# A transformer pair's head: keys and values ahead of a norm's products, a root that nobody reads, and VectorE work moved later

## The chip, the cores and the metric

The kernel runs on one core of a Trainium2 chip. The core has a matrix engine (TensorE, PE in the profile, with PEld for its weight loads), VectorE (DVE), ScalarE (ACT), GpSimd (POOL) and SyncE (SP), which issues the transfers. The metric is the device time of one execution in microseconds. All arithmetic is in 32-bit floats.

## The reference

Two blocks run one after the other on 32 sequences of 64 positions with 512 features. The first is an attention block with an MLP, both behind a root-mean-square norm whose scale depends on the sequence's condition vector; the second is a sparse attention block behind a conditioned layer norm. What this case touches is the start of the first block:

```python
n = x * rsqrt(mean(square(x), -1) + 1e-6)       # ada_rms, twice: before attention, before the MLP
h = n * (w * (1.0 + t @ tw.T))[:, None, :]
q, k, v = h @ Wq.T, h @ Wk.T, h @ Wv.T          # 8 query heads of 64, one key/value head
q, k = apply_rope(q, pos_ids), apply_rope(k, pos_ids)     # cos and sin of pos * inv_freq
x = x + (softmax(q @ k.T / 8) @ v) @ Wo.T
h = ada_rms(x, time_emb, ln2_w, ln2_tw)
x = x + (silu(h @ Wg.T) * (h @ Wu.T)) @ Wd.T
```

## The kernel before, in words

The 2048 rows are cut into eight units of 256 (four sequences each). A unit passes through `attention0`, `mlp` and `attention1`. The MLP's products use a seven-product scheme of half-sized blocks, so each weight set (gate, up or down of one of eight column groups q) needs, beside its three loaded blocks and a fourth loaded apart (`a_n`), four sums of them. These sums are formed once, while unit 0's MLP runs: `sums_of_set` (L283 to L290) does three on VectorE and the fourth on GpSimd (all four on GpSimd for sets 0 and 1). Then they are stored in DRAM for the later units (`done_with`, L292). There are five set buffers (tag `mw`) and two for `a_n` (tag `a21`), so a later load waits until an earlier set is used up.

**Order.** A scheduler places the instructions of each engine from their dependencies, and each engine runs its own list in order. In the head of the kernel TensorE's order is written by hand: the string `FIRST` (L49) is a list of turns. `a` is one step of unit 0's attention, `b` one of unit 1's, `m` one of the condition's modulation products, `i` a pair of filler products (`idle(2)`, products of a constant tile that nobody reads), `|` takes a mark. A mark is the VectorE instruction emitted last at that turn. `after(tc, engine, mark)` gives whatever is emitted inside it on that engine an order behind the mark. Sets 2 to 4 get their sums behind `marks[0]` (L280), and the rotation angles of units 2 and 3, `angles(2)`, a chain of 35 VectorE instructions and two sines, stand behind `marks[1]` (L1113). After the head the planner `Order` mixes the jobs.

**The norm in the lean form** (units 0 and 1): ScalarE squares x (`rms`, L536), VectorE and GpSimd scale x into h by the condition, TensorE sums the squares into a short tile with products against ones (`root_by_quarters`, L508), ScalarE takes the root (L505) and VectorE the reciprocal (L506); for the MLP's norm the result is spread over the partitions again by products (`row_b`, L773) and multiplied into h (L558). In unit 0 four filler products stand between the norm's products `ms_a` and the key and value products `kv` (L656 to L659). The third unit's attention (`a2`) begins with such squares too; the scheduler places them on ScalarE in the head.

ScalarE evaluates functions from tables: where the next function is in another set of tables, an ACT_TABLE_LOAD stands before it.

Of the kernel before, what the change touches and what calls it, by code (L numbers as in the profile page):

```python
# [12 lines left out]
AF = mybir.ActivationFunctionType  # L13
# [4 lines left out]
P = 128  # L18
# [26 lines left out]
TURN = (0.15911865234375, 3.628432750701904e-05, 6.4192136051133275e-09, 1.4247115856860781e-12)  # L45
ROUND = 12582912.0
WARM = 11
STAY = 14103
FIRST = "aaaaaaa bb a mm aa bb a bbb | aa b mm a bb aa a m b a bi m b ii a b |".replace(" ", "")  # L49
EARLY = 4  # L50

LAST = "aa b aa b iii b aa ii b bb bbb aaaa aa bb aaaa bbbb bb bbbb".replace(" ", "")
# [46 lines left out]
@contextmanager  # L99
def ordered(tc, engine):  # L100

    traced = tc.nc.cur_bb.bb.instructions
    start = len(traced)
    yield
    mine = [i for i in traced[start:] if i.engine == engine]
    info = mybir.DependencyInfo(mybir.DependencyClass.NoSync, mybir.DependencyReason.DATA)
    for one, other in zip(mine, mine[1:]):
        tc.add_manual_dep(other, one.name, info, reason="order")


def latest(tc, engine):
    return next(i for i in reversed(tc.nc.cur_bb.bb.instructions) if i.engine == engine)


@contextmanager
def after(tc, engine, mark):

    traced = tc.nc.cur_bb.bb.instructions
    start = len(traced)
    yield  # L120
    info = mybir.DependencyInfo(mybir.DependencyClass.NoSync, mybir.DependencyReason.DATA)
    for one in [i for i in traced[start:] if i.engine == engine]:
        tc.add_manual_dep(one, mark.name, info, reason="order")
# [3 lines left out]
def two_blocks(ctx: ExitStack, tc: tile.TileContext, a: dict, out: bass.AP):  # L127
    nc = tc.nc
# [14 lines left out]
    def abank(name):  # L143
        tags = homes["now"]
        homes["n"] += 1
        return bank(tags[homes["n"] % len(tags)], name)


    stays = {"all": const.tile([P, STAY], F32, tag="stays", name="stays"), "at": 0}

    def fixed(shape):
        n, i = int(np.prod(shape[1:])), stays["at"]
        stays["at"] += n
        assert stays["at"] <= STAY
# [16 lines left out]
    def idle(n):  # L171

        idles["n"] += 1
        ps = abank(f"idle_{idles['n']}")
        for _ in range(n):
            nc.tensor.matmul(ps[:, :P], ones, ones, start=True, stop=True)
# [12 lines left out]
    nc.gpsimd.memset(eps0, EPS0)  # L189
    eps1 = fixed([P, 1])  # L190
    nc.gpsimd.memset(eps1, EPS1)
    quarter = fixed([P, 1])
    nc.gpsimd.memset(quarter, float(np.float32(np.pi / 2)))

# [78 lines left out]
                nc.sync.dma_start(t[:, 0:4], kept[i])  # L273
            sets[n] = t

    marks = []

    def combine(n):

# [152 lines left out]
    def spread_out(ps, of):  # L432

        for b in range(US):
            nc.tensor.matmul(ps[..., b, :], spread[:, b], of, start=True, stop=True)  # L435
# [43 lines left out]
    def space(room, tag, columns, name):  # L479

        if tag in room:
            return room[tag].pop(0)[:, :columns]
        if tag == "few":
            return work({"0": "tot0", "1": "kr1"}[room["ring"]], [P, columns], name, 1)
        return work(tag + room["ring"], [P, columns], f"{name}", RING.get(tag, RING.get(tag + room["ring"], 1)))

    def tile4(room, tag, name):
        return space(room, tag, KC * UT, name).rearrange("p (c t) -> p c t", t=UT)

    def total_of(room, t, name):  # L490

        total = space(room, "tot", UT, f"tot_{name}")
        nc.gpsimd.tensor_tensor(t[:, 0:2], t[:, 0:2], t[:, 2:4], ALU.add)
        nc.gpsimd.tensor_tensor(total, t[:, 0], t[:, 1], ALU.add)
        return total

    def mean_of(parts, name):

        ps = abank(name)
        for k, part in enumerate(parts):  # L500
            nc.tensor.matmul(ps[:, :UT], ones, part, start=(k == 0), stop=(k == len(parts) - 1))
        return ps[:, :UT]

    def inverse_root(mean, eps, r):
        nc.scalar.activation(r, mean, AF.Sqrt, bias=eps)  # L505
        nc.vector.reciprocal(r, r)  # L506

    def root_by_quarters(parts, eps, r, name):  # L508

        ps = abank(name)  # L510
        for k, part in enumerate(parts):
            for b in range(US):
                nc.tensor.matmul(
                    ps[b * HALF0 : (b + 1) * HALF0, :S],
                    ones[:, :HALF0],
                    part[:, b * S : (b + 1) * S],
                    start=(k == 0),
                    stop=(k == len(parts) - 1),
                )
        inverse_root(ps[:, :S], eps, r)  # L520
# [10 lines left out]
    def rms(u, s, h, room, name):  # L531

        x = x_units[u]
        lean = "lean" in room
        sq = tile4(room, "h", f"sq_{name}") if lean else work("sq", [P, KC, UT], f"sq_{name}", 1)
        nc.scalar.activation(sq, x, AF.Square)  # L536
        if lean:
            parts = [sq[:, k] for k in range(KC)]
            c = KC // 2

            for e, part in ((nc.gpsimd if name == "a0" else nc.vector, slice(0, c)), (nc.gpsimd, slice(c, KC))):
                to = h[:, part].rearrange("p c (b s) -> p c b s", s=S)
                of = x[:, part].rearrange("p c (b s) -> p c b s", s=S)
                by = s[:, part, US * u : US * (u + 1)].unsqueeze(3).to_broadcast([P, c, US, S])
                e.tensor_tensor(to, of, by, ALU.mult)
            yield 0.0, 1.5
        else:
            parts = [total_of(room, sq, name)]
            nc.gpsimd.tensor_tensor(by_seq(h), by_seq(x), per_seq(s, u), ALU.mult)
            yield 0.0, 6.0  # L550
        if lean:
            return parts
        r = space(room, "r", UT, f"r_{name}")
        inverse_root(mean_of(parts, f"ms_{name}"), eps0, r)
        return r
# [4 lines left out]
    def project(ps, w, cols, h):  # L560
        for k in range(KC):
            nc.tensor.matmul(ps, w[:, k, cols], h[:, k, :], start=(k == 0), stop=(k == KC - 1))  # L562
# [62 lines left out]
    def attention0(u, room, early=None, late=None):  # L625
# [4 lines left out]
        def query(i):  # L630

            q = abank(f"q0_{u}_{i}").rearrange("p (c t) -> p c t", c=2)
            for c in range(2):
                project(q[:, c], wqkv[i], slice(c * P, (c + 1) * P), h)
            two = [P, 2, UT]

            def turn(cos, sin):
                cos, sin = (t.unsqueeze(1).to_broadcast(two) for t in (cos, sin))
                rotate(qT[:, 2 * i : 2 * i + 2], q, cos, sin, two, f"q0_{u}_{i}")

            return turn

        def keys_values():
            kv = abank(f"kv0_{u}")
            project(kv[:, :UT], wqkv[0], slice(2 * P, 3 * P), h)
            return kv
# [5 lines left out]
        r = yield from norm  # L652
        kv, turn = None, None
        if lean:
            few = space(room, "few", 3 * S, f"quarters_{u}").rearrange("p (k c) -> p k c", c=S)
            root_by_quarters(r, eps0, few[:, 0], f"ms_a{u}")  # L656
            if u == 0:
                idle(4)
            kv = keys_values()  # L659
            yield 1.7, 0.0  # L660
            turn = query(0)
            yield 3.4, 0.0

        if lean:
            cos, sin, r = tables_by_quarters(u, few, room)
# [9 lines left out]
        kv = kv or keys_values()  # L675
# [89 lines left out]

        h = work("h2", [P, KC, UT], f"h2_{u}", 2)
        r = yield from rms(u, s0b, h, room, f"b{u}")
        if lean:
            root = space(room, "r", UT, f"r_b{u}")[:, :S]
            root_by_quarters(r, eps0, root, f"qs_b{u}")  # L770
            yield 0.3, 2.0
            r = abank(f"row_b{u}")[:, :UT]
            spread_out(r.rearrange("p (b s) -> p b s", s=S), root)  # L773
# [336 lines left out]
    first = work("p0", [P, 1024], "p0_0", 1)  # L1110

    def later_angles():
        with after(tc, mybir.EngineType.DVE, marks[1]):  # L1113
            angles(2)

    ahead = Job(attention0(1, {"ring": "1", "lean": True}, late=later_angles), A0)
# [5 lines left out]
    with ordered(tc, mybir.EngineType.PE):  # L1122
        for name in FIRST:
            if name == "i":
                idle(2)
            elif name == "|":
                marks.append(latest(tc, mybir.EngineType.DVE))
            else:
                next(streams[name], None)
    rest = [ahead]  # L1130
# [167 lines left out]
```

## Time and profile before

| what | value |
|---|---|
| three runs | 1037.51, 1037.50 and 1035.31 us (median 1037.5) |
| profiled execution | 1038.5 us, its span 1036.7 us |
| mean granted clock of TensorE | 0.995 |
| busy: TensorE, its weight loads | 1007.9 us, 939.0 us |
| busy: VectorE, ScalarE, GpSimd | 547.7 us, 332.1 us, 437.3 us |
| moved by DMA | 198.55 MB, mean 192 GB/s |

A line of a group or a time list names the start, the duration, the engine, the line in the kernel, the operation, the tiles written and read, the shape, how many, and in brackets the idle time before it with what ended it. One fp32 product shows as two matrix records. A wait for several things is put down to the one that came last. The chain of waits is followed back from the last instruction of a stretch; its lines have a start, a duration and what ran. The lines of stretches give busy time and instruction count of PE, PEld, DVE, ACT and POOL, then the granted clock, the DMA share and GB/s.

### The profile page before, as it was taken

How to read it: one execution, taken by the hardware profiler on the slowest of the kernel's cores; microseconds unless marked ns; L12 is line 12 of the kernel's file. 1: busy time of each engine (PE TensorE's matmuls, PEld its weight loads, DVE VectorE, ACT ScalarE, POOL GpSimd, SP SyncE). 2: the span in 40 equal slices, each digit the busy share in tenths (PEclk: the TensorE clock that was granted, in tenths of full speed). 3: DMA queues.
4: the chain of work that ended last, by engine and by line, in shares of the span. 5: the costliest groups of instructions: out<-in, count | busy, mean ns of one | idle time of the engine just before them, and what ended most of it. 6: DMA issues, size and time to landing. Idle time of an engine off the chain costs nothing.

```text
span 1036.7 us, 21605 instructions
## 1 busy us (share of the span) xinstructions
PE 1007.9 (97%) x8602; PEld 939.0 (91%) x8602; DVE 547.7 (53%) x1376; ACT 332.1 (32%) x683; POOL 437.3 (42%) x522
## 2 busy tenths in 40 slices
PE   8999999999999999999999999999999999999997
PEld 7788999998999988999999989899999899999986
DVE  5876646545355376444563366552565425553274
ACT  4442112254213342143340342342333522334042
POOL 5334445444245532345342354333563343644351
PEclk9999999999999999999999999999999999999999
DMA  9736896462765463672646645446754547666201
GB/s 329 257 104 219 289 305 238 143 214 108 235 209 195 152 214 132 230 250 102 228 168 224 244 143 192 165 147 234 245 198 150 181 167 263 221 214 214 93 1 42
DMA packets 68851, 198.55 MB, mean 192 GB/s; under 512 B 7312, under 2 KB 16272, under 8 KB 68368
## 3 DMA queue, kind: packets, MB, share of 16 engines
q1 hardware_dynamic: 68752, 197.17, 55.5%
q8 instruction: 69, 1.13, 0.4%
q14 instruction: 30, 0.25, 0.1%
HBM read 180.37 MB, written 16.78 MB: 190 GB/s over the span
## 4 chain that ended last, share of the span: by engine, by line
PE 82%; DVE 8%; POOL 4%; DMA 4%; issue 2%; ACT 1%; SPq 0%; POOLq 0%; DVEq 0%; ACTq 0%
PE gu L971 33%; PE down L1030 17%; PE q L562 11%; PE po L562 8%; DMA set<-in_wmlp 2%; PE sc L906 2%; PE pp L597 2%; PE cx L933 2%; PE lat L562 1%; PE sc L720 1%; PE kv L562 1%; PE cx L741 1%; DVE sm L590 1%; PE tab L435 1%; DMA a<-in_wmlp 1%
## 5 line engine op out<-in xcount | busy, mean ns | idle before, releaser
L971 PE MATMUL gu<-h,set 128*128 128x128 f32 x2048 | 289.2, 278 | 7.8 <-DVE c L990 5.1
L971 PEld LDWEIGHTS gu<-h,set 128*128 128x128 f32 x2048 | 260.0, 193 | 16.9 <-issue 12.0
L971 PE MATMUL gu<-hc,set 128*128 128x128 f32 x1536 | 216.5, 277 | 0.0
L971 PEld LDWEIGHTS gu<-hc,set 128*128 128x128 f32 x1536 | 194.8, 193 | 1.0 <-issue 0.6
L1009 POOL TENSOR_TENSOR act<-c,c 128x384 f32<-128x384 f32 x64 | 66.5, 1039 | 212.5 <-DVE c L997 156.9
L1030 PE MATMUL down<-td,set 128*128 128x128 f32 x1024 | 137.7, 276 | 5.5 <-POOL td L1012 2.5
L1030 PEld LDWEIGHTS down<-td,set 128*128 128x128 f32 x1024 | 125.5, 192 | 7.4 <-POOL td L1012 3.4
L983 ACT COPY e<-gu 128x128 f32<-128x128 f32 x128 | 33.7, 264 | 264.5 <-PE gu L971 248.7
L1030 PE MATMUL down<-act,set 128*128 128x128 f32 x768 | 109.5, 278 | 0.3 <-DMA set<-in_wmlp 0.3
L997 DVE TENSOR_TENSOR c<-gu,u 128x256 f32<-128x256 f32 x128 | 53.3, 418 | 106.3 <-PE gu L971 106.0
L562 PE MATMUL q<-h,stays 128*128 128x256 f32 x480 | 109.1, 380 | 0.0
L562 PE MATMUL po<-cT,stays 128*128 128x256 f32 x480 | 108.2, 380 | 0.7 <-ACT cT L751 0.7
L985 DVE TENSOR_TENSOR u<-e,gu 128x128 f32<-128x128 f32 x128 | 36.0, 281 | 131.3 <-ACT e L983 130.5
L1030 PEld LDWEIGHTS down<-act,set 128*128 128x128 f32 x768 | 97.7, 192 | 5.7 <-issue 3.2
L562 PEld LDWEIGHTS q<-h,stays 128*128 128x128 f32 x480 | 89.6, 190 | 12.3 <-issue 0.4
L562 PEld LDWEIGHTS po<-cT,stays 128*128 128x128 f32 x480 | 89.3, 190 | 12.1 <-ACT cT L751 0.8
L592 POOL TENSOR_TENSOR p<-p,sm 128x512 f32<-128x512 f32 x40 | 40.9, 1042 | 120.1 <-DVE sm L591 102.6
L573 POOL TENSOR_TENSOR qT<-u_q,v_q 128x512 f32<-128x512 f32 x30 | 38.2, 1273 | 86.1 <-DVE v_q L572 86.0
L1066 ACT ACT_TABLE_LOAD x35 | 44.9, 1283 | 55.6 <-DVE c L997 55.1
L618 DVE TENSOR_TENSOR x<-x,po 128x512 f32<-128x512 f32 x28 | 19.2, 684 | 70.8 <-PE po L562 70.8
L1011 POOL TENSOR_TENSOR td<-act 128x256 f32<-128x256 f32 x64 | 46.9, 733 | 5.6 <-DVE act L1008 0.9
L1066 ACT ACTIVATE c<-gu 128x128 f32<-128x128 f32 x64 | 17.7, 277 | 84.5 <-DVE c L997 76.9
(265 smaller groups left out, 1338.2 us busy)
## 6 DMA issues: line engine op xcount, KB each, us to landing
set<-sums SPq DMA_DIRECT2D x168, 512.0 KB, 5.8
set<-in_wmlp SPq DMA_DIRECT2D x192, 384.0 KB, 4.7
sums<-set SPq DMA_DIRECT2D x24, 512.0 KB, 4.0
x<-in_x SPq DMA_DIRECT2D x8, 512.0 KB, 5.3
mod<-in_mod SPq DMA_DIRECT2D x7, 512.0 KB, 7.2
a<-in_wmlp SPq DMA_DIRECT2D x24, 128.0 KB, 3.0
out_x<-x SPq DMA_DIRECT2D x12, 256.0 KB, 2.4
stays<-in_wo SPq DMA_DIRECT2D x2, 1024.0 KB, 6.7
```

Of the source, the lines that this page charges most:

```text
L562: nc.tensor.matmul(ps, w[:, k, cols], h[:, k, :], start=(k == 0), stop=(k == KC - 1))
L573: nc.gpsimd.tensor_tensor(dst, u, v, ALU.add)
L592: nc.gpsimd.tensor_tensor(p8, p8, sm.unsqueeze(2).to_broadcast(wide), ALU.mult)
L597: nc.tensor.transpose(pp[:, c, :], p[:, c * P : (c + 1) * P], ident)
L971: nc.tensor.matmul(ps, w[:, slot, k * P : (k + 1) * P], b[of][:, k], start=start and k == 0, stop=k == 1, skip_group_check=True)
L983: nc.scalar.copy(e, ps[:, 0])
L985: nc.vector.tensor_tensor(u2, e, ps[:, 1], ALU.add)
L997: nc.vector.tensor_tensor(c.rearrange("p (a b) t -> p a b t", b=2)[:, :, 1], ps[:, 2:4], u2.unsqueeze(1).to_broadcast([P, 2, HT]), ALU.add,)
L1009: nc.gpsimd.tensor_tensor(act[:, 1:4], gate[:, 1:4], c[:, 1:4], ALU.mult)
L1011: nc.gpsimd.tensor_tensor(td[:, 0:2], act[:, 1:3], act[:, 0:2], ALU.subtract)
L1030: nc.tensor.matmul(sums_of[u][p][:, c], w[:, slot, c * P : (c + 1) * P], b[of], start=q % NP == 0 and i % 2 == 0 and c == 0, stop=q % NP = ...
L1066: nc.scalar.activation(gate[2][:, 0], gate[0][:, 0], AF.Silu)
```

## The change

Seven edits, all but one in the head of the kernel.

- In unit 0 the four filler products and the key and value products are emitted ahead of `root_by_quarters`, which sums the squares.
- A new turn `r` in `FIRST`, behind the last scores of unit 1, emits a square root of one column on ScalarE into a new column `root`, in order behind the ScalarE instruction emitted last. Nobody reads it. STAY, the columns of the fixed tile, grows by one.
- `roots` records this root and then the ScalarE instruction emitted last in `root_by_quarters` of units 0 and 1; the squares of `a2` get an order behind the latest of them, unit 1's.
- In `FIRST` the first `|` goes and the second stands one turn earlier, so `marks[0]`, behind which sets 2 to 4 are summed, is the last VectorE instruction of unit 0's norm before its MLP.
- One filler pair `i` goes.
- `angles(2)` gets its order behind the VectorE instruction emitted last when it is called, at the end of unit 1's norm, instead of `marks[1]`.
- `kv` is formed where it is unless it was already.

```diff
-STAY = 14103
-FIRST = "aaaaaaa bb a mm aa bb a bbb | aa b mm a bb aa a m b a bi m b ii a b |".replace(" ", "")
+STAY = 14104
+FIRST = "aaaaaaa bb a mm aa bb a bbb aa b mm a bb r aa a m b a bi m b i a | b".replace(" ", "")
...
+    root = fixed([P, 1])
...
-        nc.scalar.activation(sq, x, AF.Square)
+
+        with after(tc, mybir.EngineType.Activation, roots[-1]) if name == "a2" else nullcontext():
+            nc.scalar.activation(sq, x, AF.Square)
...
+            if u == 0:
+
+                idle(4)
+                kv = keys_values()
             root_by_quarters(r, eps0, few[:, 0], f"ms_a{u}")
-            if u == 0:
-                idle(4)
-            kv = keys_values()
+            kv = kv or keys_values()
...
             root_by_quarters(r, eps0, root, f"qs_b{u}")
+            roots.append(latest(tc, mybir.EngineType.Activation))
...
-        with after(tc, mybir.EngineType.DVE, marks[1]):
+        with after(tc, mybir.EngineType.DVE, latest(tc, mybir.EngineType.DVE)):
             angles(2)
...
+            elif name == "r":
+                with after(tc, mybir.EngineType.Activation, latest(tc, mybir.EngineType.Activation)):
+                    nc.scalar.activation(root, quarter, AF.Sqrt)
+                roots.append(latest(tc, mybir.EngineType.Activation))
```

More of the change, by code (lines that the diff above doesn't have):

```diff
@@ L274, in load_sets @@
             sets[n] = t
-    marks = []
+    marks, roots = [], []
     def combine(n):
@@ L655, in attention0 @@
             few = space(room, "few", 3 * S, f"quarters_{u}").rearrange("p (k c) -> p k c", c=S)
-            root_by_quarters(r, eps0, few[:, 0], f"ms_a{u}")
             if u == 0:
                 idle(4)
-            kv = keys_values()
+                kv = keys_values()
+            root_by_quarters(r, eps0, few[:, 0], f"ms_a{u}")
+            kv = kv or keys_values()
             yield 1.7, 0.0
```

## The prediction

> **What bounds the kernel now.** I read the page's busy shares first, then the chain of waits for the first 150 us (the change touches nothing later), then TensorE's instructions in order of time with the idle time before each, and last the stretches with their granted clock.
>
> ```profile
> PE 1007.9 (97%) x8602; PEld 939.0 (91%) x8602; DVE 547.7 (53%) x1376; ACT 332.1 (32%) x683; POOL 437.3 (42%) x522
> ```
>
> TensorE is busy 1007.9 of 1036.7 us, so all there is to win is 28.8 us of idle time, filler products, and products at half clock. The chain from the end of unit 0's attention to its first MLP product:
>
> ```profile
> 53.59 0.56 DVE x L618
> 54.18 1.06 ACT sq_b L536
> 55.26 0.27 ACT rows L337
> 55.53 0.49 ACT pT L598
> 56.02 0.95 ACT sq_a L536
> 56.99 1.28 ACT L505
> 58.28 0.32 ACT r_b L505
> 58.63 0.56 DVE r_b L506
> ```
>
> Between the squares the norm needs (sq_b) and its root (r_b), ScalarE does two things that nothing there needs: sq_a, the squares of the third unit, and a table load (the L505 line without a name). They cost 0.95 + 1.28 us. In TensorE's own list:
>
> ```profile
> 10.94 1.08 PE L513 MATMUL ms_a<-sq_a,stays 128*32 128x64 f32 x32 [1.43 <-ACT sq_a L536]
> 11.95 2.08 PE L176 MATMUL idle<-stays 128*128 128x128 f32 x8
> 13.82 2.01 PE L562 MATMUL kv<-h,stays 128*128 128x256 f32 x8
> ...
> 61.79 2.06 PE L971 MATMUL gu<-h,set 128*128 128x128 f32 x8 [0.48 <-DVE h L558]
> ...
> 83.46 1.16 PE L1030 MATMUL down<-td,set 128*128 128x128 f32 x8 [2.16 <-DVE x L618]
> ```
>
> At 83.46 a PSUM bank is still held by an output sum that VectorE adds late (L618), 2.16 us of idle TensorE. The clock (the number after POOL's):
>
> ```profile
> 12.00:15.00 3.00, 3.00 (x16) 2.89 (x14) 0.56 (x3) 2.96 (x9) 0.74 (x5) 0.66 1.08 377
> 63.00:66.00 3.00, 3.00 (x18) 2.97 (x18) 1.89 (x7) 0.05 (x1) 0.00 (x0) 0.63 0.08 22
> ```
>
> Two stretches at about half clock follow thinly filled ones. Near 63 a gu product takes some 0.23 us a record (1.82 for 8), later 0.11 (1.06 for 8).
>
> **The change part by part**, against the profiled execution: 1038.5 us, of which 1036.7 are span and 1.8 lie around it. It is 1.0 us above the median of the three runs (1037.5; lowest 1035.3).
>
> 1. *Keys and values ahead of the norm's products.* In the changed kernel's compiled order the four fillers that stood behind ms_a do not stay there: one goes before the first modulation product and three behind the first pair of fillers, so eight more records stand before the second modulation block, which now starts at 7.68 because its load lands then. At 0.22 us (half clock) until 7.2 and 0.11 after, the block starts near 8.15: +0.45, and with it the s0a vector and POOL's h_0 (which ends at 12.03, so 12.5). kv then runs behind each half of h_0 (1.8 us in all) and ends near 13.4, ms_a adds 0.6, and q starts near 14.0 instead of 15.8: -1.8. The root behind ms_a is still released by ScalarE's table load (ends 14.7), its reciprocal and scaling are over by about 16, and the tables need it at 17.5: covered by q, 1.5 us to spare. Downstream POOL is late next: set 0's sums start when their load lands (19.13, four at 0.73), and the compiled order now puts one sum of set 1 ahead of the first rotation, so the rotations gain 0.3 and 0.9 and the scores 1.4 at most. The other bound: TensorE now idles from about 9.2 to 11.5 with one transpose in it, and if the clock halves behind that, kv and q lose 1.7 us and the part ends 1.4 us worse. I take -0.6, ends -1.4 and +1.4.
>
> [...] The trace drops the clock for 3.4 us behind a stretch with 1.6 us of idle time (8.75 to 9.21 and 9.50 to 10.6). [...]
>
> 2. *The set sums of sets 2 to 4 leave VectorE's queue between 41.8 and 51.7* (nine instructions, 6.7 us, one behind a load that lands at 45.8). What do they hold up? Output products run on TensorE from 45.6 to 52.7 whatever VectorE does. Only the end is worth something: L618 ends at 54.15 where the product ends at 52.7 and the add takes 0.6, so -0.8.
>
> 3. *Third unit's squares go behind unit 1's root, the table load behind the last exponential* (an unread root of one column). The load then lies in ScalarE's idle time ahead of sq_b (3.34 us, against 1.28 + about 0.3). From sq_b's end to r_b's end it was 3.36 us; rows 0.27, pT 0.5 and the root 0.31 remain: -2.3. [...] But TensorE's order lies behind it: contexts 0.6, two fillers, transpose and four transposes 1.1, one filler pair 0.5 (the change takes out the other pair) stand ahead of row_b, and these now end last. That gives back 1.0.
>
>    Parts 2 and 3: -0.8 - 2.3 + 1.0 = -2.1. The squares' new place is ScalarE's idle 1.69 us at 95 to 96.7 (needs 1.06), their two POOL sums (1.26 + 0.72) fit POOL's idle 2.93 us before 98.72. Without that cover each would delay the activation, and so the down products, by about a microsecond.
>
> 4. *The half-clock stretch at 61.8 to 65.2* costs 16 records at 0.22 instead of 0.11, 1.7 us. With parts 2 and 3, TensorE's gaps ahead of it (0.94, 0.52, 0.24, 0.48) mostly close. But windows move: -0.9, ends -1.7 and 0.
>
> 5. *The angles leave 63.4 to 82.8* (35 VectorE instructions, 10.7 us busy), the nine set sums come in there, 3.7 us without contention. The compiled order then has L618 behind the sums of sets 5 and 6 and six evacuations. Set 5's load is issued when the first gate set is used up and lands 3.7 us later, as now; from there I get the add done just when TensorE's last output product is, so the 2.16 us shrink to about 0.1: -2.1. If the sums land late, all of it stays: end 0. On SP the loads of wq1, wkd, wkv1, x and wo1 no longer stand behind a_4, whose issue waited for VectorE until 43.6; a_4, a_5, a_6 and three 512 KB stores move into 61 to 68, where DMA was idle (share 0.02 to 0.08). The fifth VectorE sum waits for a_4, whose load can be issued only behind set 2's sums: about 0.4 us, and the activations behind it are not yet due.
>
> 6. *The angles' new place is q = 3 and 4 of unit 0's MLP* (103 to 119 of the old time), among sums and evacuations in the same queue. Interleaved they cost 0.20 us each (start to start). Following the compiled order from 103.3: the gate's evacuation of q = 3 ends 0.2 later (two sums moved behind it), the up's 1.4 later, and TensorE waits there 1.2 more. The next sums wait for their load until 112.82:
>
> ```profile
> 109.42 0.28 DVE L1008 TENSOR_TENSOR act<-c,gu 128x128 f32<-128x128 f32 x1
> 112.82 0.42 DVE L287 TENSOR_TENSOR set<-a,set 128x256 f32<-128x256 f32 x1 [3.12 <-DMA set<-in_wmlp]
> ```
>
>    Those 3.12 us swallow what is left of the first half; in q = 4 two more sums have moved behind the gate's evacuation, and TensorE is 1.1 late at 118. Some of it is absorbed by later waits for loads (0.79, 0.26, 0.51, 0.32 at 127 to 146). I take +0.9, ends -0.3 and +3.5 (half of the 35 at 0.20 on TensorE's path).
>
> Sum: -0.6 - 2.1 - 0.9 - 2.1 + 0.9 = -4.8, from 1038.5 to 1033.7 us, 3.8 under the median.
>
> **Rivals.**
> (a) *The loads take it back.* From 105 to 165 the DMA share is 0.8 to 1.0, and VectorE waits 16.8 us for sets between 62 and 150. If bytes and not freed buffers set that stretch, TensorE arrives early and waits: 1037.5. Against it: between 80 and 90 the share is about 0.5, and each set load is issued as TensorE frees a buffer, so the stretch should start earlier too.
> (b) *The clock halves elsewhere*: part 1 at +1.4 and part 4 at 0, hence 1033.7 + 2.0 + 0.9 = 1036.6.
> (c) *Slower: the angles hold the set sums.* VectorE's queue is in order; behind each late sum stands the next a-load on SP, and behind that the stores and set loads. With its idle time gone (loads landing earlier), all 35 at 0.26 us, the spacing where they run alone, go onto TensorE's path: 9.1 instead of 0.9, 1041.9. It decides from 6.8 us on. For it: L990 already ends TensorE's waits at 105.6, 107.5, 116.0 and 127.7. Against it: the 3.12 us above, and 4.50 at 134.5.
> (d) *Part 1 doesn't do what it says*: fillers merely move ahead of the modulation, gain 0 there: 1034.3, within the likeliest case.
> (e) *Everything at its good end* (-1.4, -1.7, -0.3): 1030.9 or lower.
>
> **How the numbers follow.** The likeliest case, with (d) in it, has 0.70 and its own range 1031.5 to 1035.4; (a) 0.08, (b) 0.08, (c) 0.09, (e) 0.05. About 0.2%, 2.1 us, is what a measurement of this kernel can tell from no change. Faster: 0.67 of the 0.70, the 0.05, and 0.01 of (b), 0.73. Same: 0.03, most of (a) and (b), 0.15. Slower: (c) and the upper part of (a), 0.12. The range reaches from (e)'s end to beyond (b): 1030.8 to 1037.2.
>
> **What would show it.** kv ahead of ms_a and q at 14 to 15; a table load between the last exponential and sq_b, the root straight behind pT; the first gu product near 58.3 at full clock (60 if not); no wait at down's second bank; up's evacuation of q = 3 more than a microsecond late. Wrong if TensorE idles more between 95 and 160 than now, or if kv runs at half clock.

## The result, and the profile after

The changed kernel takes 1032.4 us (median of 11 runs, 1030.1 to 1034.7) against 1036.7 us (11 runs, 1033.4 to 1039.0) of the kernel before, measured beside it: 0.9966 of the time, 95% interval 0.9949 to 0.9982. That is 4.3 us faster, where 3.8 were forecast; the range held it. Its profiled execution took 1034.7 us, of which 1032.7 are span; before, it was 1038.5 and 1036.7. The two spans differ by 4.0, and I compare them event by event.

The page of the changed kernel, busy time by engine:

```profile
PE 1004.3 (97%) x8598; PEld 935.9 (91%) x8598; DVE 547.4 (53%) x1376; ACT 332.2 (32%) x684; POOL 437.4 (42%) x522
```

TensorE still sets the end: it is busy 3.6 us less (1007.9 before) and idle 0.4 us less. One stretch at half clock less (1.7 us) and the filler pair that the change takes out (0.45 us) are part of the 3.6. The busy time of the others is what it was.

The chain of waits of the changed kernel from the end of unit 0's attention to its first MLP product (start, duration, what ran):

```profile
53.22 0.70 DVE x L621
...
53.94 1.06 ACT sq_b L539
...
55.29 0.50 ACT pT L601
...
55.83 0.76 PE cx L746 x8
...
58.23 0.85 PE row_b L436 x8
...
60.45 1.16 PE gu L977 x8
```

The third unit's squares and the table load are gone from it, but the root is gone too: behind pT the chain now leaves ScalarE for TensorE's own list (contexts, fillers, a transpose, then row_b). Where the load and the root went is in ScalarE's list of the changed kernel, in order of time (with idle time before an instruction and what ended it in brackets):

```profile
49.14 1.28 ACT L1136 ACT_TABLE_LOAD   x1
50.43 0.20 ACT L1136 ACTIVATE stays<-stays 128x1 f32<-128x1 f32 x1
53.94 1.06 ACT L539 ACTIVATE sq_b<-x 128x1024 f32<-128x1024 f32 x1 [3.31 <-DVE x L621]
...
55.78 0.31 ACT L506 ACTIVATE r_b<-qs_b,stays 128x64 f32<-128x64 f32 x1
```

The load lies in ScalarE's idle time, and from the end of sq_b (55.00) to the end of the root r_b (56.09) it takes 1.1 us, against 3.36 before. Each of the two traces has 80 such loads of 1283 ns, ahead of roots, exponentials, SiLUs and, at the start, an absolute value and a sine, and none ahead of a copy or a square; the two sines at 81.98 us of before run between SiLUs without one. At the norms' roots there were 23 of the 80; now there are 22, and one at the unread root. TensorE's list of the changed kernel:

```profile
12.01 3.48 PE L565 MATMUL kv<-h,stays 128*128 128x256 f32 x8 [1.57 <-POOL h L548]
15.42 0.65 PE L514 MATMUL ms_a<-sq_a,stays 128*32 128x64 f32 x32
16.00 3.72 PE L565 MATMUL q<-h,stays 128*128 128x256 f32 x16
...
60.45 1.16 PE L977 MATMUL gu<-h,set 128*128 128x128 f32 x8 [0.79 <-DVE h L561]
...
77.73 1.66 PE L1036 MATMUL down<-td,set 128*128 128x128 f32 x12
79.22 1.06 PE L977 MATMUL gu<-h,set 128*128 128x128 f32 x8
...
104.06 1.13 PE L977 MATMUL gu<-h,set 128*128 128x128 f32 x8 [1.61 <-DVE prod L383]
...
115.61 1.13 PE L977 MATMUL gu<-h,set 128*128 128x128 f32 x8 [1.50 <-DVE ang L393]
```

Keys and values do run ahead of ms_a, but in 3.48 us, mostly at half clock, and q starts at 16.00, later than before (15.66). The first gate product (gu) starts 1.34 us earlier and takes 1.16 us for eight records where it took 2.06. The wait of 2.16 us at down's second bank is gone. In its place stand two waits at q = 3 and q = 4: an evacuation (VectorE taking a finished product out of PSUM) stands there behind the angles in VectorE's queue. The clock (the number after POOL's busy time) in the stretches of the changed kernel that answer to those shown of before:

```profile
12.00:15.00 3.00, 2.99 (x7) 2.46 (x8) 2.00 (x5) 1.63 (x6) 2.11 (x6) 0.50 1.05 377
63.00:66.00 3.00, 3.00 (x17) 2.69 (x16) 2.97 (x9) 0.27 (x1) 1.57 (x2) 1.00 0.55 197
```

The stretch in the head is still at half clock; the one near 63 us is gone. So, from profile to profile (after less before, running total at the same event):

| event | before | after | total | step |
|---|---|---|---|---|
| tables of unit 0 (tab) | 19.11 | 19.56 | +0.45 | +0.45 |
| second output sum of unit 0 (L618, now L621) starts | 53.52 | 53.22 | -0.30 | -0.75 |
| root r_b starts | 58.28 | 55.78 | -2.50 | -2.2 |
| first gate product | 61.79 | 60.45 | -1.34 | +1.16 |
| first gate product behind down's second bank | 84.46 | 79.22 | -5.24 | -3.9 |
| squares of unit 1's norm summed (qs_b) | 93.93 | 88.84 | -5.09 | +0.15 |
| up product of q = 4 | 117.40 | 115.61 | -1.79 | +3.3 |
| exponentials' transposes at 246 (pp) | 249.17 | 245.75 | -3.42 | -1.6 |
| last output products | 1026.27 | 1022.33 | -3.94 | -0.5 |

The -3.9 is the wait of 2.16 us and the 1.7 us of the half-clock stretch near 63.

### The profile page after: what moved, and what is told of

Its sections match the earlier page's. It is cut to its first block, busy times and chain, and to the rows that moved or that the text cites. A ratio compares the mean times of both kernels' runs of the same rounds, so it can differ in the third digit from the quotient of the medians.

```text
span 1032.7 us, 21599 instructions
## 1 busy us (share of the span) xinstructions
PE 1004.3 (97%) x8598; PEld 935.9 (91%) x8598; DVE 547.4 (53%) x1376; ACT 332.2 (32%) x684; POOL 437.4 (42%) x522
## 4 chain that ended last, share of the span: by engine, by line
PE 84%; DVE 6%; POOL 4%; DMA 2%; issue 2%; ACT 1%; SPq 0%; POOLq 0%; DVEq 0%; ACTq 0%
PE gu L977 34%; PE down L1036 17%; PE q L565 11%; PE po L565 9%; PE sc L912 2%; PE pp L600 2%; PE cx L939 2%; PE lat L565 1%; DMA set<-in_wmlp 1%; PE kv L565 1%; PE sc L725 1%; PE cx L746 1%; PE tab L436 1%; DMA mod<-in_mod 1%; DVE sm L593 1%
## 5 line engine op out<-in xcount | busy, mean ns | idle before, releaser
L1072 ACT ACT_TABLE_LOAD x35 | 44.9, 1283 | 54.9 <-DVE c L1003 54.4
L621 DVE TENSOR_TENSOR x<-x,po 128x512 f32<-128x512 f32 x28 | 19.2, 687 | 72.8 <-PE po L565 72.8
```

The lines of the kernel that those rows point to most:

```text
L1072: nc.scalar.activation(gate[2][:, 0], gate[0][:, 0], AF.Silu)
```

## The experiments

Two readings of each kernel are given. One is the median of its runs and its ratio to the kernel before, run beside it. The other takes out the clock: every run lists its mean granted clock, and over 304 runs (128 of the kernel before) a least-squares fit of time on clock, with one level for each kernel, gives 8.3 us for each 0.01 of mean clock. The level of a kernel less that of before is what the kernel does at equal clock (+/- is 95%); a gain that comes by a better clock is not in it. The clock is listed to 0.001, and 0.001 is 0.8 us. The medians of before were 1037.3 (62 runs, beside e1 to e4), 1036.8 (43 runs, beside e5 to e8) and 1036.9 us (23 runs, beside e9 to e12); at equal clock these three groups differ by 0.1 us at most.

| kernel | median us | ratio, 95% | at equal clock |
|---|---|---|---|
| the change (first runs; again: e9) | 1032.4; 1032.9 | 0.9966; 0.9959, 0.9945 to 0.9973 | -3.6 +/- 0.5 |
| e1 keys and values ahead, alone | 1036.6 | 0.9992, 0.9977 to 1.0006 | -0.6 +/- 0.5 |
| e2 unread root and later squares, alone | 1034.7 | 0.9976, 0.9965 to 0.9987 | -2.1 +/- 0.4 |
| e3 sums and angles moved, alone | 1035.1 | 0.9979, 0.9966 to 0.9991 | -1.8 +/- 0.4 |
| e11 sums moved, alone | 1036.5 | 1.0001, 0.9989 to 1.0013 | +0.3 +/- 0.5 |
| e12 angles moved, alone | 1035.0 | 0.9985, 0.9972 to 0.9999 | -1.5 +/- 0.5 |
| e8 change without keys and values ahead | 1032.5 | 0.9956, 0.9944 to 0.9968 | -3.8 +/- 0.8 |
| e4 change, fillers held | 1032.4 | 0.9953, 0.9939 to 0.9967 | -3.8 +/- 0.5 |
| e7 change, no angles | 1031.9 | 0.9949, 0.9935 to 0.9964 | -3.3 +/- 0.8 |
| e10 change, fillers held, no angles | 1031.4 | 0.9947, 0.9931 to 0.9963 | -4.5 +/- 0.7 |
| e5 change, angles early | 1037.6 | 1.0009, 1.0001 to 1.0017 | -0.3 +/- 0.4 |
| e6 change, angles early, fillers held | 1036.7 | 1.0003, 0.9995 to 1.0012 | -0.5 +/- 0.4 |

### Each part alone (e1, e2, e3)

e1: the kernel before with part 1 only.

```diff
-            root_by_quarters(r, eps0, few[:, 0], f"ms_a{u}")
             if u == 0:
                 idle(4)
-            kv = keys_values()
+                kv = keys_values()
+            root_by_quarters(r, eps0, few[:, 0], f"ms_a{u}")
+            kv = kv or keys_values()
```

> The kernel before with the first part alone: unit 0's fillers and key and value products ahead of the norm's products. If the part is a small gain on average, as predicted (-0.6 us, ends -1.4 and +1.4): about 1036 us against 1036.7; the rotation tables start between 17.7 and 20.5 us against 19.1 in the profile of before, early where kv runs at full clock and late where it runs at half. If the part carries the change (rival): 1033 to 1034 and the first gu product 3 us or more ahead of 61.8.

Measured: 1036.6 us, 0.9992 (0.9977 to 1.0006): in the times no difference that can be told from none, at equal clock 0.6 +/- 0.5 faster. That is the forecast size, but the forecast way to it is missing: the profile has no half clock in the head and still starts the tables at 18.06, later than every full-clock profile of the old order (17.08 to 17.77 in e2, e3, e8, e11 and e12). Where the gain lies is shown under e11 and e12.

e2: the kernel before with the unread root and the third unit's squares behind unit 1's root; both pairs of fillers stay.

```diff
-FIRST = "aaaaaaa bb a mm aa bb a bbb | aa b mm a bb aa a m b a bi m b ii a b |"
+FIRST = "aaaaaaa bb a mm aa bb a bbb | aa b mm a bb r aa a m b a bi m b ii a b |"
...
-        nc.scalar.activation(sq, x, AF.Square)
+        with after(tc, mybir.EngineType.Activation, roots[-1]) if name == "a2" else nullcontext():
+            nc.scalar.activation(sq, x, AF.Square)
...
+            elif name == "r":
+                with after(tc, mybir.EngineType.Activation, latest(tc, mybir.EngineType.Activation)):
+                    nc.scalar.activation(root, quarter, AF.Sqrt)
```

> The kernel before with the unread root and the third unit's squares behind unit 1's root, nothing else. Theory: from the end of sq_b to the end of r_b 1.1 to 1.6 us instead of 3.4, the first gu product 1 to 1.5 us earlier than 61.8 (TensorE's own order then ends last), the wait at down's second bank stays near 2 us because VectorE still has the angles in front of the output sum: 1035 to 1035.7. Rival (all of the gain in the head comes from here): first gu product 3 us earlier and 1033.5.

Measured: 1034.7 us, 0.9976; 2.1 us at equal clock. TensorE's list of e2 shows how little of the root's gain reaches the gate product directly:

```profile
56.34 1.06 PE L176 MATMUL idle<-stays 128*128 128x128 f32 x8
57.24 1.00 PE L436 MATMUL row_b<-r_b,stays 128*128 128x64 f32 x8
...
59.62 1.16 PE L975 MATMUL gu<-h,set 128*128 128x128 f32 x8 [0.79 <-DVE h L561]
...
79.13 1.16 PE L1034 MATMUL down<-td,set 128*128 128x128 f32 x8 [1.58 <-DVE x L621]
```

The root ends at 54.8 there, row_b begins at 57.24, and between them TensorE is not idle: among others twelve filler records stand in its list, the last eight of them shown. The change takes four of the twelve out. The wait at down's second bank is still there with 1.58 us, 0.6 shorter than before.

e3: the kernel before with the set sums behind unit 0's norm and the angles behind unit 1's.

```diff
-FIRST = "aaaaaaa bb a mm aa bb a bbb | aa b mm a bb aa a m b a bi m b ii a b |"
+FIRST = "aaaaaaa bb a mm aa bb a bbb aa b mm a bb aa a m b a bi m b ii a | b"
...
-        with after(tc, mybir.EngineType.DVE, marks[1]):
+        with after(tc, mybir.EngineType.DVE, latest(tc, mybir.EngineType.DVE)):
             angles(2)
```

> The kernel before with the marks moved alone: sums of sets 2 to 4 behind unit 0's norm, angles behind unit 1's norm. Theory: sq_b 0.7 us earlier, no wait at down's second bank (-2.1), two waits of about 1.5 us for the up evacuations at q = 3 and 4, of which half comes back by 140 us (+1.6): 1035.4 in all. Rival (the loads take it back): the gain at 84 us is gone by 150 and the time is 1036.7.

Measured: 1035.1 us, 0.9979; 1.8 us at equal clock. No wait stands at down's second bank; two waits for the angles (1.73 and 1.70 us) stand at q = 3 and 4.

e2 and e3 add up: -2.1 - 1.8 = -3.9 against the change's -3.6 +/- 0.5. Part 1 is not needed in that sum, and with e1's -0.6 it would come to -4.5.

### Which of the two moves (e11, e12)

e11 moves only the sums, e12 only the angles.

```diff
-FIRST = "aaaaaaa bb a mm aa bb a bbb | aa b mm a bb aa a m b a bi m b ii a b |"
+FIRST = "aaaaaaa bb a mm aa bb a bbb aa b mm a bb aa a m b a bi m b ii a | b |"
```

> The kernel before with only the nine set sums moved behind unit 0's norm; the angles stay where they were. The prediction's step 2 has this gain 0.8 us ahead of the first gate product. But the sums then stand with the angles in VectorE's queue from 61 to 83 us, 3.7 us more work ahead of the output sum that TensorE waits for at down's second bank: that wait grows from 2.16 to 3 or more, and the time is 0 to 2 us above the kernel before, 1037.5 to 1039. If the 63 to 83 us stretch had room for both (the rival), it is 0.8 us faster, 1036.4.

```diff
-        with after(tc, mybir.EngineType.DVE, marks[1]):
+        with after(tc, mybir.EngineType.DVE, latest(tc, mybir.EngineType.DVE)):
             angles(2)
```

> The kernel before with only the angles moved behind unit 1's norm; the nine set sums stay early. By the prediction's terms: the wait of 2.16 us at down's second bank goes, and 0.9 comes back at q = 3 and 4: 1.2 us faster. By the profile of both moves together (2.2 us faster): if the angles alone carry it, 1035.1; then the sums' move is worth nothing by itself and only the angles' leaving counts. If the sums' move is needed too, less than half of it, 1036.5.

Measured: 1.0001 for the sums, 0.9985 for the angles (-1.5 +/- 0.5, against -1.8 for both). So the angles' leaving carries the step, and the sums' move alone is worth nothing that shows; what it adds to the angles' (e3 less e12) is -0.3 +/- 0.6. TensorE's list of e11, where both share VectorE from 61 to 83 us:

```profile
70.36 1.13 PE L971 MATMUL gu<-h,set 128*128 128x128 f32 x8 [1.16 <-DVE c L990]
81.53 1.16 PE L1030 MATMUL down<-td,set 128*128 128x128 f32 x8 [2.11 <-DVE x L618]
```

I had expected the second wait to grow to 3 or more; it stayed at 2.11, and a new wait of 1.16 us came up at 70, for an evacuation behind the sums.

What each part does ahead of the gate product can be read almost without noise: the distances between the starts of unit 0's output products (po), of the squares sq_b and of the first gate product (gu) repeat to 0.02 us in profiles of the same order.

| profile | po to sq_b | sq_b to gu |
|---|---|---|
| before; e12 (angles) | 8.61; 8.60 | 7.61; 7.61 |
| e11 (sums); e3 (sums and angles) | 7.93; 7.93 | 7.61; 7.60 |
| e1 (keys and values ahead) | 7.93 | 7.61 |
| e2 (root, all fillers) | 8.59 | 6.95 |
| the change; e8; e9 | 7.93; 7.93; 7.93 | 6.51; 6.50; 6.51 |

So the sums' move is worth 0.68 us at the gate product and the root 0.66; the filler pair that goes with it adds 0.44. In e11 the 0.68 is won at the gate product and lost again at 70 us.

e1 has the 7.93 too, with the sums where they were. VectorE's list says why, first before, then e1 (L287 is a set sum, L582 belongs to the softmax):

```profile
45.80 0.93 DVE L287 TENSOR_TENSOR set<-a,set 128x256 f32<-128x256 f32 x1 [0.15 <-DMA a<-in_wmlp]
46.66 0.74 DVE L582 TENSOR_REDUCE mx<-sc 128x4 f32<-128x256 f32 x2
```

```profile
44.51 0.74 DVE L582 TENSOR_REDUCE mx<-sc 128x4 f32<-128x256 f32 x2
47.94 1.26 DVE L287 TENSOR_TENSOR set<-a,set 128x256 f32<-128x256 f32 x1
```

In e1's compiled order the sum that waited for its load stands behind the softmax's work instead of ahead of it, and from the first of these set sums to the second output sum VectorE takes 11.04 us instead of 11.76. So what e1 gains is a by-product on VectorE and not the step that was forecast, and the change, which moves these sums away anyway, cannot gain it a second time.

### Part 1 and the clock (e4, e8, e9)

e4: the change with the fillers, six instead of four, held between the modulation's transpose and the keys and values, so that TensorE's gap there is filled.

```diff
-                idle(4)
+                with after(tc, mybir.EngineType.PE, latest(tc, mybir.EngineType.PE)):
+                    idle(6)
                 kv = keys_values()
```

> The changed kernel with six fillers held between the modulation's transpose and kv instead of four that the scheduler hoists ahead of the modulation. Theory: the modulation is not delayed (second block at 7.7 instead of 8.6), TensorE does not go thin before kv, so kv runs at full clock, ends near 14 and the tables start near 17.5 to 18 instead of 19.6: 1.2 to 1.8 us under the changed kernel, about 1031. Rival (the clock halves whatever the fillers do, or POOL's set sums hold the rotations): scores of unit 0 no earlier than 29, time 1032.4.

e8: the change without part 1, that is with the diff of e1 undone. e9: the change as it is, again.

> The changed kernel without its first part: the norm's products, then the fillers, then keys and values, as before. The prediction's step (keys and values ahead gain 0.6 us) gives 1033.0. The profiles of the first runs say otherwise: with keys and values ahead the rotation's tables start at 18.06 without a half-clock stretch (against 17.35 and 17.63 in the old order) and at 19.56 with one (against 19.11), so the first part costs 0.4 to 0.7 us and this kernel takes 1031.9, tables at 17.4 or 19.1. If the first part is neutral, 1032.4.

> The changed kernel itself, once more, beside the next three, so that they stand on one chip and one set of runs of the kernel before. Expected as on record: 0.996 to 0.9966 of the time before, 1032.4 to 1033.

Measured: 1032.4, 1032.5 and 1032.9 us, ratios 0.9953, 0.9956 and 0.9959. The three cannot be told apart: no gain of part 1 shows in the change, and none of filling the gap (mean clock of e4 0.9978, against 0.9979 of the change). Why is seen where the head runs at full clock. First TensorE in e8 (old order), then in e9 (the change):

```profile
10.57 0.65 PE L514 MATMUL ms_a<-sq_a,stays 128*32 128x64 f32 x32 [0.74 <-ACT sq_a L539]
11.15 1.16 PE L176 MATMUL idle<-stays 128*128 128x128 f32 x8
12.15 1.89 PE L565 MATMUL kv<-h,stays 128*128 128x256 f32 x8
13.88 3.62 PE L565 MATMUL q<-h,stays 128*128 128x256 f32 x16
17.33 1.05 PE L436 MATMUL tab<-quarters,stays 128*128 128x128 f32 x8
```

```profile
8.63 1.07 PE L330 MATMUL ps_mod<-mod,stays 128*32 128x128 f32 x28
10.15 0.30 PE L343 MATMUL pt_mod<-stays,rows 128*128 128x128 f32 x1 [0.46 <-ACT rows L338]
12.02 2.13 PE L565 MATMUL kv<-h,stays 128*128 128x256 f32 x8 [1.57 <-POOL h L548]
14.08 0.65 PE L514 MATMUL ms_a<-sq_a,stays 128*32 128x64 f32 x32
14.66 3.72 PE L565 MATMUL q<-h,stays 128*128 128x256 f32 x16
18.22 1.05 PE L436 MATMUL tab<-quarters,stays 128*128 128x128 f32 x8
```

In the old order ms_a and the fillers lie in the time in which TensorE waits for h anyway; kv ends at 14.04 and 14.15. In the new order that time is empty (1.57 us), ms_a stands behind kv, and the modulation's second block starts 0.6 later behind the hoisted fillers. So q starts 0.8 and the tables 0.9 us later. Over all profiles with a full-clock head the tables start at 17.4 on average in the old order (five profiles, 17.08 to 17.77), at 18.1 in the new one (e1, e5 and e9, 18.04 to 18.22) and at 17.9 with the fillers held (e4, e6 and e10). Half clock in the head shows in two of five profiles of the new order (the first and e7), in one of six of the old (before) and in none of three with held fillers: too few to say whether the order changes how often it comes. The loss at the tables does not show in the times: e8 less the change is -0.2 +/- 0.9 at equal clock, too wide to exclude it.

### The angles' new place (e5, e6, e7, e10)

e7 and e10 leave the angles of units 2 and 3 out of the change (a constant stands in for them): e7 from the change, e10 from e4. They measure the whole price of the angles where they now stand.

```diff
-            angles(2)
+            nc.vector.memset(angle[:, :, 2 * S : 4 * S], 0.5)
+            positions.pop()
+            load_positions(4)
```

> The changed kernel without the angles of units 2 and 3: their products on VectorE and their two table functions are left out, and a constant stands in their place, so that the rotations of these two units use other angles. It measures the whole price of the angles in their new place. By the record of the changed kernel (TensorE 3.2 us late by 116 to 118 us, about 1.6 us of it made good by 140): 1.6 us faster than the change, 1030.8. By the prediction's term (+0.9): 1031.5. If later loads take the whole loss back: 1032.4, the same. If the rival held in which all 35 stand on TensorE's path: 9 us faster, 1023.

> The changed kernel with the six fillers held, and without the angles of units 2 and 3 (a constant stands in their place, so the rotations of these two units use other angles): the price of the angles once more, with a head at full clock in the profiled execution. Theory (the set loads pace TensorE from 100 to 150 us, and the angles' waits only stand in place of waits for loads): the waits of 1.6 and 1.7 us behind the angles are gone, TensorE is ahead at 116 us by 1 to 3 us against the kernel with held fillers, waits for set loads or for their sums from 105 to 150 us come in their place, and at 150 us it is ahead by less than 0.5; the time stays within 0.5 us of the change. Rival (the angles' price is real): ahead by 1.5 us or more at 150 us and in the median, 1030.9 or lower.

Measured: e7 1031.9 us, at equal clock 0.3 +/- 0.8 above the change; e10 1031.4 us, 0.7 +/- 0.8 below e4 and 0.9 +/- 0.8 below the change. The two readings differ, with six runs each: the price is at most about 1.7 us and may be nothing, though the two waits for the angles come to 3.1 us in the changed kernel's profile and to 3.3 in e4's. TensorE's list of e10:

```profile
100.54 1.13 PE L978 MATMUL gu<-h,set 128*128 128x128 f32 x8 [0.31 <-DVE c L997]
107.81 1.58 PE L1037 MATMUL down<-td,set 128*128 128x128 f32 x12 [0.33 <-DVE set L289]
...
138.52 0.71 PE L1037 MATMUL down<-act,set 128*128 128x128 f32 x4 [0.39 <-DMA set<-in_wmlp]
```

and VectorE's there, where the changed kernel has it busy without a break:

```profile
106.57 0.42 DVE L288 TENSOR_TENSOR set<-a,set 128x256 f32<-128x256 f32 x1 [3.79 <-DMA set<-in_wmlp]
```

At q = 3, where e4 waits 1.61 us for the angles (102.21), TensorE of e10 waits 0.31 (100.54); then it waits for sets and for sums of sets that have not landed. Counted from each one's first gate product, it is 1.5 us ahead of e4 at the up product of q = 3, 1.6 at that of q = 4 and 0.2 at the exponentials' transposes (pp) near 243 us. In this pair of profiles the loads take back most of what the angles cost.

e5 puts the 35 products where VectorE seemed idle, behind the unread root at 49 us, with another buffer (`r1`) for the intermediate product; e6 is e5 with the fillers held.

```diff
-    def angles(u0):
+    def angles(u0, ring="r0"):
...
-        prod = some("r0", "prod", UT, 1)
+        prod = some(ring, "prod", UT, 1)
...
+                with after(tc, mybir.EngineType.DVE, latest(tc, mybir.EngineType.DVE)):
+                    angles(2, "r1")          # at turn r
...
-    ahead = Job(attention0(1, {...}, late=later_angles), A0)
+    ahead = Job(attention0(1, {...}, late=None), A0)
```

> The changed kernel with the angles' products issued right behind the early root, into VectorE's idle time at 49 to 59 us, instead of behind unit 1's norm. If the new place of the angles (among the set sums of q = 3 and 4) is what gives time back, the two waits of 1.61 and 1.50 us of TensorE for the up part's evacuations go, no work of the angles stands in q = 3 and 4 any more, and the kernel gains what of the 3.2 us did not come back by itself, 1.5 us: 1030.9. The rival (late loads absorb the whole loss by 146 us, so the place costs nothing in the end) gives no change against the changed kernel, 1032.4. A third outcome: the 35 products interleave with the norm's scaling behind the root of unit 0, at 0.2 us each, and the first gate product starts later than 60.5 by 1 us or more: then 1033.4 or worse.

> The angles early and the six fillers held behind the modulation transpose, together. If both are separate gains (keys and values at full clock in the profiled execution with the fillers held; no waits at q = 3 and 4 with the angles early), they add: 1030.9 less 0 to 1.0, so 1030 to 1031. If holding the fillers does nothing to the median (it gave 1032.4, as the change itself), the result is that of the early angles alone.

Measured: 1037.6 and 1036.7 us, ratios 1.0009 and 1.0003: the whole gain of the change is lost. The third outcome that I had written down came, and worse than priced. VectorE in e5, then GpSimd, TensorE and the stretch with its clock:

```profile
53.01 1.09 DVE L383 TENSOR_SCALAR prod<-ang 128x128 f32<-128x128 f32 x1
54.13 1.83 DVE L378 TENSOR_SCALAR stays<-prod 128x128 f32<-128x128 f32 x1
...
60.46 0.23 DVE L378 TENSOR_SCALAR stays<-prod 128x128 f32<-128x128 f32 x1
60.60 1.21 DVE L561 TENSOR_TENSOR h<-h,row_b 128x1024 f32<-128x1024 f32 x1
```

```profile
52.97 1.04 POOL L548 TENSOR_TENSOR h<-x,stays 128x512 f32<-128x512 f32 x1 [2.32 <-DVE x L621]
53.97 1.90 POOL L552 TENSOR_TENSOR h<-x,stays 128x1024 f32<-128x1024 f32 x1
```

```profile
58.59 1.08 PE L436 MATMUL row_b<-r_b,stays 128*128 128x64 f32 x8 [1.38 <-DVE prod L379]
...
61.87 1.14 PE L977 MATMUL gu<-h,set 128*128 128x128 f32 x6 [1.61 <-DVE h L561]
```

```profile
63.00:66.00 3.00, 3.00 (x11) 2.44 (x10) 3.00 (x13) 0.00 (x0) 0.95 (x1) 0.52 0.00 0
```

A product that takes 0.2 to 0.3 us elsewhere took 1.09 and 1.83 us here. Each of the two ran beside one of GpSimd's instructions and ended within 0.1 us behind it, which speaks for the two engines being in each other's way; no run takes that apart. From po to the first gate product e5 takes 17.37 us where the change takes 14.44: TensorE idled twice (1.38 and 1.61 us), and the clock was 0.52 from 63 to 66 us behind it. Down's second bank waits for L621 again, 0.95 us. The waits at q = 3 and 4 did shrink (to 0.37 at most), but loads were waited for (0.69 and 0.27 us at 134 and 145). At equal clock e5 is 3.3 +/- 0.6 above the change, the 2.9 us ahead of the gate product among them; the rest of its 5 us is clock (a mean of 0.9959 against 0.9979).

## Why the prediction was right, and where it was not

The forecast of 1033.7 us and its sign came true, but both signs that it had named for being wrong came up too: in the profiled execution kv ran at half clock, and between 95 and 160 us TensorE idled 4.81 us where it had idled 2.98. They belong to terms 1 and 6. Where the sum had -0.6, -2.1, -0.9, -2.1 and +0.9, the two profiles have +0.45 at the tables, -1.8 to the gate product, -3.9 to behind down's second bank (1.7 of it the clock, 2.2 the wait that went), and +1.3 from there to the end: -3.9.

So terms 1, 2 and 3, and 6 came out 1.05, 0.3 and 0.4 us worse, and the clock term 0.8 better. That last one is luck: a half-clock stretch that the profile of before happened to have. The sum without its clock term is -3.9, and -3.3 without part 1 too; the runs at equal clock give -3.6 +/- 0.5. So parts 2, 3, 5 and 6 carry the result.

1. *Keys and values ahead, -0.6: wrong.* It measured +0.45 at the tables between the two profiles, about +0.7 between the full-clock profiles of both orders, and no gain in the times of the change. The -0.6 between its ends (-1.4 and +1.4) was my estimate; no run shows it. That e1 gains 0.6 at equal clock is the right number by luck: it comes from VectorE's order. The step that failed is "q starts near 14.0 instead of 15.8". The 14.0 was a start at full clock and the 15.8 one at half clock: I booked the half-clock stretch of the profile before to the order of the products. At full clock the old order starts q at 13.88 (e8) and the new one at 14.66 (e9). The second failing is the bound: I had the fillers hoisted and the gap of some two microseconds opened in the forecast itself, and put the halving behind it at the bad end only (+1.4); in the profiled execution it came (clock 0.50 from 12 to 15 us), in e9 behind the same gaps it did not (1.00). The root behind ms_a was costed wrongly too, without effect. ScalarE's list of the changed kernel:

```profile
16.18 1.28 ACT L506 ACT_TABLE_LOAD   x1 [2.24 <-PE ms_a L514]
```

   ScalarE was free from 13.94, but the load waited until ms_a was done (15.42 + 0.65), and the root followed at 17.48. I had the load end at 14.7, with 1.5 us to spare. Not every load waits so: in unit 1's norm it ran from 87.85, ahead of the sums (qs_b, from 88.84) that its root needs.

2. *Sums out of VectorE's queue, -0.8: right at the place, not by itself.* It measured -0.68 from po to sq_b. What the step left out is what the sums delay where they go: with the angles still there, an evacuation at 70 us takes it back, and e11 stands at +0.3 +/- 0.5. Part 5 clears that place, but that the 0.68 then counts the times do not show (e3 less e12, -0.3 +/- 0.6).

3. *Squares and table load, -2.3, with 1.0 given back to TensorE's order: right at the gate product.* From sq_b's end to the root's end it fell from 3.36 to 1.1 us, and of the 2.27 TensorE's own list ahead of row_b gave back 1.17: 1.10 remain from sq_b to gu, the filler pair's 0.44 among them. Parts 2 and 3 together measure -1.78 at the gate product, against -2.1. The load cost what its row shows, 1.28 us, and nothing stood between it and the root, before (56.99 + 1.28, root at 58.28) or after (49.14 + 1.28, root at 50.43). The "58.3" that I named for the gate product at full clock did not agree with my own sum, which has 59.1 (61.79 - 2.7); e9 shows 59.12, but 0.9 of that comes from its full-clock head and not from part 1. By the runs the part alone is worth 2.1 us, more than the 1.3 of the sum; its profile shows 0.66 at the gate product and 0.6 at down's second bank, and where the rest comes from I did not settle.

   The moved squares found their cover, some 5 us earlier than I had put it (89.78 instead of 95), and the table load behind them waited for its input, 0.75 us idle.

4. *The half-clock stretch near 63, -0.9 (ends -1.7 and 0).* Between the two profiles it was the full 1.7. But e1, e3, e11 and e12, in which TensorE's gaps ahead of the gate product are as before, show no half clock there either (1.16 us for the eight records): that the change removed it is not shown. Over all runs the mean clock rose from 0.9972 to 0.9979, which at 8.3 us for 0.01 is 0.6 +/- 0.6 us. The -0.9 lies within that. "Windows move", by which the term took about half of the 1.7, was my estimate: no run shows a window. What the runs show is half clock that comes in one execution and not in another (kv 3.48 and 2.13 us in two profiles of the changed kernel); by which gaps it comes stays open.

5. *The angles leave 63 to 83 us, -2.1: right.* The wait of 2.16 is gone; e12, which moves nothing else, has it gone too and gains 1.5 +/- 0.5, with term 6 in it.

6. *The angles' new place, +0.9 (ends -0.3 and +3.5): right on the whole, wrong at the spot.* TensorE waits 1.61 at q = 3 and 1.50 at q = 4, as said for q = 3, and is 3.3 later by 117; I had +1.1. "Those 3.12 us swallow what is left of the first half" failed: sums and evacuations of q = 4 came into VectorE's queue before the wait for the set could take anything up. But 1.6 came back by 246 us, 0.9 of it in waits behind q = 4 that were shorter than before (0.95 us against 1.88). From down's second bank to the end the term is +1.3, and without any angles the kernel gains 1.7 at most.

Rival (c), by which the angles' 35 products all stand on TensorE's path for 9.1 us, is excluded by e7 and e10. Rival (a), in which the loads take back all, is true of the stretch from 100 to 150 us in part: it returns some of what is lost there and takes some of what is gained, but not the gains made ahead of it. Rival (d), no gain of part 1, is what the times of e8 show as far as they can tell. The first half of rival (b), the clock halving behind part 1, came in the profiled execution; over all runs the clock did not get worse. Rival (e), everything at its good end, fits only the three runs at clock 1.0 (1030.1 to 1030.5), not the median.

## What to carry to other kernels

Before an order is priced, put both sides at the same clock: a stretch at half clock in one profile may belong to that execution and not to the order of the products (kv of the changed kernel took 3.48 us in one profile and 2.13 in the next). A wait in a stretch paced by loads can cost a fraction of its length (3.1 us of waits were worth 1.7 at most here), so leave a whole piece of work out once to see its full price before looking for a better place. An engine's idle time next to a chain that sets the end looks free and need not be: 49 to 59 us was the dearest of the three places that VectorE's angles had here (e5, 3.3 us above the change at equal clock).

## What I had not expected of the hardware

The clock halves or not in the same kernel, behind the same gaps. In the changed kernel's first profile and in its second (e9) TensorE idles 0.46 and 1.57 us before kv; in the first, kv takes 3.48 us, in the second 2.13. Near 246 us the same, first profile and then e9:

```profile
245.75 0.44 PE L600 MATMUL pp<-stays,p 128*128 128x128 f32 x2 [1.92 <-POOL p L595]
...
247.54 1.91 PE L977 MATMUL gu<-h,set 128*128 128x128 f32 x8
```

```profile
244.37 0.44 PE L600 MATMUL pp<-stays,p 128*128 128x128 f32 x2 [1.92 <-POOL p L595]
...
246.88 1.06 PE L977 MATMUL gu<-hc,set 128*128 128x128 f32 x8
```

The clock from 12 to 15 us is 0.50 in the first profile and 1.00 in e9; from 247.5 to 250.9 us it is 0.55 in the first, and in e9 it is 1.00 from 244 to 252. So the length of the gaps alone (2.03 us before kv, 1.92 at 246) does not decide it; what does, no run shows. The clock also goes with most of the spread between runs: over the 128 runs of before it accounts for 74% of the variance. Grouped by their clock, the runs of before go from 1034.9 us (clock 1.0, 19 runs) to 1040.3 (0.993, 8 runs), and those of the change from 1030.4 (1.0, 3 runs) to 1034.7 (0.995 and 0.996, one each).

The waits where loads arrive differ between executions, too. Behind q = 4 TensorE waits 0.59 and 0.36 us in the changed kernel's first profile, both times for an evacuation, and in e9 0.23 us for an evacuation and 0.51 for the sums of a set. e7's profiled execution took 1036.5 us (clock 0.997) where its other five runs lie between 1030.2 and 1034.1 (0.998 to 1.0); from 110 to 145 us its TensorE waited 1.02 us for sets and 1.66 for sums of sets, where the changed kernel's first profile, with the angles in it, lists no such wait. A difference of about a microsecond between two single profiles in that stretch is no evidence by itself here.
